# Layer 0: the choice behind GpSimd's norm tile and its last step in two places; the last half's factors on VectorE

## The chip, the cores and the metric

The kernel runs on one core of a Trainium2 chip. A core has five engines that work at the same time: TensorE (PE, with its weight loads as PEld), VectorE (DVE), ScalarE (ACT), GpSimd (POOL) and SyncE (SP), which issues the DMAs here. Each takes its own instructions in order and waits on semaphores for the others. The metric is the time of one execution on the device in microseconds (us), lower is better; shown is the median of several runs.

## The reference

Four pairs of layers work on x of 8 x 512 tokens, 128 wide, all in float32; each adds its result to x, after a norm over the 128 columns. The kernel splits x into 8 batches of 512 tokens. Two of the eight layers are touched.

Layer 0's second half is a mixture of 16 experts with the two best taken, for each token and each of 8 heads (16 columns each):

```python
h = x @ Wm + bm
t = h.reshape(bs * L_ * H, HD)
logits = t @ expert_emb
w = jax.nn.softmax(logits, axis=-1)
topw, topi = jax.lax.top_k(w, K)
hmid = jax.nn.gelu(jnp.einsum('td,edi->tei', t, W1) + b1, approximate=False)
eo = jnp.einsum('tei,eio->teo', hmid, W2) + b2
sel = jnp.take_along_axis(eo, topi[:, :, None], axis=1)
comb = (sel * topw[:, :, None]).sum(axis=1)
return comb.reshape(bs, L_, d) @ Wo + bo
```

Layer 3's second half rounds its inputs to a 4-bit grid in blocks of 16 values, each block with a factor of its own:

```python
scale = jnp.maximum(jnp.max(jnp.abs(xb), axis=-1, keepdims=True) / 6.0, 1e-12)
xn = xb / scale
idx = jnp.searchsorted(_MID, jnp.abs(xn))
q = _GRID[idx] * jnp.sign(xn) * scale
...
gate = fp4_linear(x, w_gate)
y = fp4_linear(x, w_up)
h = jax.nn.silu(gate) * y
return fp4_linear(h, w_down)
```

## The kernel before

The order of the instructions on every engine is the order in which the program writes them (a manual schedule). Layers 0 and 1 run first, then layers 2 and 3 together in one long loop of frames, and the last batch of layer 3 after it, written out by hand in `end()`.

**Layer 0, pass two.** A list of stages, each with a lag, is run for i from -4 to 10, and a stage works on batch i + lag. `turned` (L365-370) turns a normed batch on TensorE and copies it on ScalarE; `scale` (L353-358) norms a batch, three tiles of 128 tokens on ScalarE and the fourth on GpSimd (L358); `stats` gets the norm's factors, with three small operations on GpSimd (L246, L247, L763); `biased` (L361) adds a bias to a whole batch on GpSimd; `spikes` multiplies on GpSimd (L401); `logits` (L445, L446) and `attended` (L274) are VectorE's; `exponentials` is ScalarE's (L449). `keep_clock(n)` (L840) puts n matmuls without a use on TensorE.

**The choice.** `choice(b)` (L451-496) is a generator: it finds the best two of 16 experts for each token and head, with a yield after each step. Most steps are one VectorE instruction on 128 x 512 (L458 to L479); two of them have one on GpSimd behind them (L469, L473). The last steps write the weights: four products, one for each of 128 tokens (L484), in one step; then a transpose on VectorE (L489) and four DMAs to DRAM (`plain`, L492). For batch 0 it is advanced three steps at a time by `chosen(3)` in pass two; `chosen(20)` behind it takes what is left.

**Layer 0, the loop.** 128 units (8 batches x 16 experts) follow. `first_half` makes a hidden activation: matmuls, then two gelus on ScalarE (L594, L595). `second_half`, two units later, multiplies back on TensorE, takes the weights `gs` on VectorE (L607) and adds on GpSimd (L611). `gs` is loaded by SP: a block is four experts, in eight DMAs; `twice` writes the weights of a batch to DRAM twice (`gates`), three units after its choice was stored, and the blocks are read from there; only block 0 of batch 0 comes from `plain` itself, in 16 DMAs. Three buffers hold blocks. The matmuls of `second_half` share one PSUM bank, which L607 frees.

After each `second_half`, `side("V", n)` advances one step of a generator (in units 0 to 5: 4, 2, 1, 2, 1 and 2 steps): the choice of the next batch, if its time has come (from unit 16(b-1)-9 on; batch 1 at once), or else `others()`, which makes layer 1's index tables (`places`) and the norm of layer 1's first batches (`first_norms`). When a generator ends, that takes a slot too. The last step of `first_norms` turns batch 0 on TensorE (L826) and copies it on VectorE (L828); it waits at "P", the slot ahead of the second half, which there is in units 0 to 127 alone. What is left is run behind the loop. Layer 1 begins with the projection of this batch.

**The end.** Batch 7 of layer 3 is done in two halves, A (tokens 0 to 255) and B (256 to 511); L is batch 6, of which the last parts lie among theirs. For each tile of 128 tokens, `gated` multiplies by the gate's and the up weights and takes a tanh on ScalarE (L2158); `gated_v` forms the product on VectorE (L2164), and, with `at_end` and `thirds`, copies the other factor on ScalarE (L2161) and takes the last product on GpSimd (L2166), without `thirds` on VectorE (L2168). `quant_h1` (L1401 to L1406) gets the blocks' factors; `fp4_round` (L1409-1429) rounds: two instructions make a mask (L1418, L1421), one adds it, one subtracts it (L1422, L1423), and GpSimd multiplies by the factors (L1424). `turn_h` turns on TensorE (L2216) and copies on ScalarE (L2219), `down` multiplies back into one PSUM bank, adds to x on VectorE (L2100) and stores by SP (L2239). `bank()` hands out two PSUM banks in turn (tag "one"); `bank("c")` is one of its own, which half A's convolution used before.

Of the kernel before, what the change touches and what calls it, by code (L numbers as in the profile page):

```python
# [17 lines left out]
F32 = mybir.dt.float32  # L18
I32 = mybir.dt.int32
# [145 lines left out]
def body(ctx, tc, dram, spans, x_in, ib, it, ic, ei, out):  # L165
# [23 lines left out]
    def bank(tag="one"):  # L189
        if tag == "one" and "own" in banks:  # L190
            return banks["own"]
        return banks["pool"].tile([P, TB], F32, tag=tag, name="ps1", bufs=banks["tags"][tag])
# [94 lines left out]
    def layer0():  # L287
# [7 lines left out]
        with ExitStack() as st:  # L295
# [64 lines left out]
            def biased(b, bias):  # L360
                nc.gpsimd.tensor_tensor(  # L361
                    x[b], x[b], bc[bias].unsqueeze(1).to_broadcast([P, J, D]), ALU.add
                )
# [87 lines left out]
            def choice(b):  # L451


                d = by_expert(depth, b)
                ex = acc[b].rearrange("p (g e) -> p g e", e=16)
                place, top, sm = small("place"), small("top"), small("sm")
                eq, one, left = big("eq"), big("one"), big("left")
                nc.vector.scalar_tensor_tensor(eq, d, 0.0, rank, ALU.is_equal, ALU.mult)  # L458
                yield "V"
                nc.vector.tensor_reduce(place, eq, AX.X, ALU.max)  # L460
                yield "V"
                nc.vector.tensor_tensor(one, eq, over(place), ALU.is_equal)
                yield "V"
                nc.vector.scalar_tensor_tensor(left, one, -1e30, d, ALU.mult, ALU.add)
                yield "V"
                nc.vector.tensor_reduce(top, left, AX.X, ALU.max)
                yield "V"
                nc.vector.tensor_tensor(eq, left, over(top), ALU.is_equal)
                nc.gpsimd.tensor_tensor(eq, eq, rank, ALU.mult)  # L469
                yield "V"  # L470
                nc.vector.tensor_reduce(sm, ex, AX.X, ALU.add)
                nc.vector.reciprocal(sm, sm)
                nc.gpsimd.tensor_tensor(ex, ex, over(sm), ALU.mult)  # L473
                yield "V"
                nc.vector.tensor_reduce(place, eq, AX.X, ALU.max)
                yield "V"
                nc.vector.tensor_tensor(one, eq, over(place), ALU.is_equal)
                yield "V"
                nc.vector.scalar_tensor_tensor(left, one, -1e30, left, ALU.mult, ALU.add)  # L479
                yield "V"  # L480
                by_e = one.rearrange("p g e -> p (g e)").rearrange("p (j e h) -> p j h e", j=J, h=8)
                for j in range(J):
                    r = slice(8 * j, 8 * (j + 1))
                    nc.vector.scalar_tensor_tensor(  # L484
                        by_e[:, j, :, :], left[:, r, :], -1e29, ex[:, r, :], ALU.is_le, ALU.mult
                    )
                yield "V"
                g = big("turned").rearrange("p g e -> p (g e)")
                nc.vector.transpose(g, one.rearrange("p g e -> p (g e)"))  # L489
                to = plain[b].rearrange("(c r) (j a s) -> a r j c s", c=4, j=J, a=4)  # L490
                for a in range(4):
                    nc.sync.dma_start(  # L492
                        to[a], g[32 * a : 32 * (a + 1), :].rearrange("r (j c s) -> r j c s", j=J, c=4)
                    )
                (written.add if b == 0 else stored.setdefault)(b)
                yield "V"
# [8 lines left out]
            def chosen(n):  # L505
                for _ in range(n):
                    next(first_choice, None)

            with (
                tc.tile_pool(name="a0h", bufs=1) as hp,  # L510
                tc.tile_pool(name="a0", bufs=2) as ap,
                psum({"one": 8}),
                tc.manual_schedule(),
            ):
                hs = [hp.tile([P, NB, TB], F32, tag=f"h{k}", name=f"h{k}") for k in range(3)]
                bst = [hp.tile([P, NB, 6], F32, tag=f"bst{k}", name=f"bst{k}") for k in range(3)]

                def run(stages, iterations):
                    for i in iterations:
                        for f, lag in stages:  # L520
                            if 0 <= i + lag < NB:
                                f(i + lag)

                run(
                    (
                        (scale, 2),
                        (stats, 3),
                        (turned, 1),
                        (project, 0),
                        (lambda b: biased(b, "bp"), -2),  # L530
                    ),
                    range(-3, NB + 2),
                )
                keep_clock(22)
                sc, bi = batch_norm()
                expand()
                run(
                    (
                        (turned, -2),
                        (scale, -1),  # L540
                        (turn_v, 3),
                        (logits, -3),
                        (attended, 0),
                        (stats, 0),
                        (spikes, 4),
                        (gram, 2),
                        (gram_out, 1),
                        (hidden, -2),
                        (exponentials, -3),
                        (lambda b: chosen(3), -4),  # L550
                        (lambda b: biased(b, "bo"), -1),
                        (lambda b: keep_clock(6), -3 - NB // 2),
                    ),
                    range(-4, NB + 3),
                )
                chosen(20)
# [852 lines left out]
    def fp4_round(pool, dst, sc, a, blocks, room=None):  # L1409

        shape = [P, blocks, 16]
        room = room or blocks
        m = pool.tile([P, room, 16], F32, tag=f"fm{room}", name="fm")[:, :blocks, :]
        nc.vector.tensor_scalar(  # L1418
            m.bitcast(I32), a.bitcast(I32), 0x7F800000, None, ALU.bitwise_and
        )  # L1420
        nc.vector.tensor_scalar(m, m, 1.0, 1.5 * 2.0**22, ALU.max, ALU.mult)  # L1421
        nc.vector.tensor_tensor(a, a, m, ALU.add)  # L1422
        nc.vector.tensor_tensor(a, a, m, ALU.subtract)  # L1423
        nc.gpsimd.tensor_tensor(  # L1424
            dst.rearrange("p (n k) -> p n k", k=16),
            a,
            sc.unsqueeze(2).to_broadcast(shape),
            ALU.mult,
        )
# [3 lines left out]
    def late():  # L1433
# [11 lines left out]
        with tc.tile_pool(name="a2", bufs=2) as wp, tc.tile_pool(name="l3", bufs=1) as lp:  # L1445
# [584 lines left out]
            def layer3(b, xp, tile_, part=(0, J), conv_bank="one", h_tag="h"):  # L2030
# [68 lines left out]
                def added(ps):  # L2099
                    nc.vector.tensor_tensor(  # L2100
                        x[b][:, j0:j1, :],
                        x[b][:, j0:j1, :],
                        ps[:, lo:hi].rearrange("p (j d) -> p j d", d=D),
                        ALU.add,
                    )
# [78 lines left out]
                def quant_h2(i):  # L2184
                    fp4_round(lp, pair(i), *t["fh", i], 44)

                def quant_h2_tile(i, j):
                    sc, a = t["fh", i]
                    k = slice(22 * j, 22 * (j + 1))
                    h = tile_("h", h_tile)  # L2190
                    fp4_round(lp, h[:, 2 * i + j, :], sc[:, k], a[:, k, :], 22)

                def blocks_h(i):
                    m = lp.tile([P, 44, 16], F32, tag="fm44", name="hb")
# [26 lines left out]
                        )  # L2221

                def down():
                    ht = tile_("ht", None)
                    po = bank()
                    for j in range(j0, j1):
                        for k, _ in thirds:
                            mm(
                                cols(po, j),
                                ht[:C3, j, k, :],  # L2230
                                wt["down"][:C3, k, :],
                                start=(j == j0 and k == 0),
                                stop=(j == j1 - 1 and k == 2),
                            )
                    added(po)
                    stored()

# [147 lines left out]
            def end():  # L2385
# [48 lines left out]
                B.quant_x1()  # L2434
                A.gated_v(1)
                B.quant_x2()
                L.down()
                keep_clock(6)
                B.turn_x()
                B.gated(2, True)  # L2440
                B.gated(3, True)
                A.quant_h1(0)
                A.quant_h2(0)
                B.gated_v(2)
                B.gated_v(3)
                keep_clock(8)
                B.quant_h1(1)
                A.turn_h(0)
                B.quant_h2_tile(1, 0)
                B.quant_h2_tile(1, 1)  # L2450
                A.down()
                keep_clock(22)
                B.turn_h(1)
                B.down()

# [290 lines left out]
```

## Time and profile before

| | |
|---|---|
| median of 3 runs | 1390.49 us (1388.63 to 1393.59) |
| the profiled execution | 1387.75 us, its span 1385.6 us |
| instructions | 33142 |
| busy: PE, DVE, ACT, POOL | 1323.9, 1024.1, 1011.0, 646.3 us |
| pass two of layer 0 | about 44 to 101 us |
| loop of layer 0 | 101 to 380 us: PE 273.75 and ACT 270.45 busy of 280 |
| the end, from the last frame on | about 1323 to 1385.6 us |

The profile is of one execution. Busy shares are averages over stages with different limits, so each stage is read by itself: the timeline of an engine lists its instructions with start, duration and, in brackets, the time that the engine was idle before and what ended it. A busy PE is not PE at its peak, as its matmuls' ends are modelled.

### The profile page before, as it was taken

The numbers are of one execution on the slowest core, as the hardware profiler recorded it, in microseconds if no ns is written. First come the engines' busy times: TensorE is split into PE (matmuls) and PEld (weight loads), VectorE is DVE, ScalarE is ACT, GpSimd is POOL, SyncE is SP. The second block draws the span as 40 slices with busy tenths as digits, with TensorE's granted clock in tenths as the row PEclk, the third lists the DMA queues.
The fourth block names the chain that finished last, engine by engine and source line by source line (L and its number), as shares of the span: only waits on it lengthen the run. The fifth ranks groups of instructions, "written<-read, shape, count | busy, mean of one in ns | idle before, by whom it ended". The sixth has DMA issues, their size and how long they took to land.

```text
span 1385.6 us, 33142 instructions
## 1 busy us (share of the span) xinstructions
PE 1323.9 (96%) x12910; PEld 704.4 (51%) x12910; DVE 1024.1 (74%) x2173; ACT 1011.0 (73%) x2050; POOL 646.3 (47%) x758
## 2 busy tenths in 40 slices
PE   7889999999989899999999999999999999999997
PEld 3762222222277655547447455555555555555576
DVE  6786666677477778863783689788788897887876
ACT  6859999999977656655684686777767767667632
POOL 6756667765632533230472453453443634424432
PEclk9999999999999999999999999999999999999999
DMA  5015555555280111241201101102011010110000
GB/s 181 1 25 163 170 145 149 150 152 145 62 278 28 28 40 35 65 115 30 73 21 36 45 2 22 31 2 43 11 23 23 9 33 20 23 23 10 2 9 16
DMA packets 125309, 84.47 MB, mean 61 GB/s; under 512 B 61984, under 2 KB 103712, under 8 KB 124769
## 3 DMA queue, kind: packets, MB, share of 16 engines
q1 hardware_dynamic: 123423, 78.43, 20.3%
q0 software_dynamic: 1152, 2.36, 0.6%
q8 instruction: 102, 1.67, 0.5%
q10 hardware_dynamic: 578, 1.57, 0.3%
q14 instruction: 54, 0.44, 0.1%
HBM read 64.29 MB, written 22.23 MB: 62 GB/s over the span
## 4 chain that ended last, share of the span: by engine, by line
PE 37%; DVE 14%; ACT 10%; issue 2%; POOL 1%; DMA 0%; DVEq 0%; ACTq 0%; POOLq 0%
PE ps L250 27%; PE ps L1598 8%; ACT ex L1677 6%; DVE nm L1671 5%; ACT prod L2065 2%; DVE acc L2051 1%; PE ps L2248 1%; DVE fa L1422 1%; DVE fa L1406 1%; ACT q L1559 1%; DVE fsc L1401 1%; ACT xn L1481 1%; DVE fa L1423 1%; DVE fm L1418 1%; DVE k L1560 1%
## 5 line engine op out<-in xcount | busy, mean ns | idle before, releaser
L1677 ACT ACTIVATE ex<-ps,nm 128x512 f32<-128x512 f32 x512 | 345.2, 687 | 172.3 <-DVE nm L1671 172.2
L1671 DVE TENSOR_REDUCE nm<-ps 128x2 f32<-128x1024 f32 x256 | 300.9, 1210 | 39.1 <-PE ps L250 39.0
L250 PE MATMUL ps<-q,k 64*64 64x512 f32 (+1 forms) x2240 | 258.3, 564 | 8.9 <-ACT ex L1677 5.7
L250 PE MATMUL ps<-ex,vs 128*64 128x512 f32 x1024 | 233.8, 598 | 1.1 <-DVE sm L1691 1.1
L1692 POOL TENSOR_TENSOR vs<-v,sm 128x256 f32<-128x256 f32 x128 | 78.6, 614 | 292.9 <-DVE sm L1691 268.6
L1598 PE MATMUL ps<-xt,blob_a 64*64 64x512 f32 x912 | 207.8, 589 | 0.1
L611 POOL TENSOR_TENSOR acc<-acc,pr 128x512 f32<-128x512 f32 x120 | 165.9, 1382 | 87.2 <-DVE pr L607 78.8
L595 ACT ACTIVATE hm<-ps,blob_f 128x1536 f32<-128x1536 f32 x128 | 196.2, 1533 | 0.0
L607 DVE SCALAR_TENSOR_TENSOR pr<-ps,blob_f,gs 128x512 f32<-128x512 f32 x120 | 90.0, 750 | 87.2 <-PE ps L250 76.6
L250 PEld LDWEIGHTS ps<-q,k 64*64 64x64 f32 x2240 | 74.8, 132 | 152.0 <-ACT ex L1677 78.2
L250 PE MATMUL ps<-h,w 32*128 32x512 f32 x1024 | 148.3, 643 | 1.1 <-ACT hm L594 0.6
L250 PEld LDWEIGHTS ps<-ex,vs 128*64 128x64 f32 x1024 | 68.0, 136 | 152.9 <-issue 128.1
L250 PE MATMUL ps<-hm,w 128*32 128x512 f32 x1024 | 136.8, 606 | 5.1 <-DVE pr L607 2.7
L2066 POOL TENSOR_TENSOR acs<-acs,prod 128x512 f32<-128x512 f32 x96 | 124.0, 1292 | 23.9 <-ACT prod L2065 19.4
L1598 PE MATMUL ps<-blob_a,ct 64*64 64x128 f32 x1824 | 118.6, 269 | 0.0
L1598 PE MATMUL ps<-blob_a,xt 64*64 64x128 f32 x1824 | 118.5, 269 | 0.0
L1598 PEld LDWEIGHTS ps<-blob_a,ct 64*64 64x64 f32 x1824 | 106.2, 133 | 0.0
L1677 ACT ACTIVATION_READ_ACCUMULATOR ex<-ps,nm 128x1 f32 x512 | 105.0, 205 | 0.0
L1598 PEld LDWEIGHTS ps<-blob_a,xt 64*64 64x64 f32 x1824 | 103.0, 133 | 0.0
L250 PEld LDWEIGHTS ps<-h,w 32*128 32x128 f32 x1024 | 41.1, 183 | 108.7 <-ACT hm L594 103.4
L594 ACT ACTIVATE hm<-ps,blob_f 128x512 f32<-128x512 f32 x128 | 88.0, 687 | 8.5 <-PE ps L250 8.3
L1598 PEld LDWEIGHTS ps<-xt,blob_a 64*64 64x64 f32 x912 | 61.7, 133 | 31.9 <-issue 28.4
(366 smaller groups left out, 2212.3 us busy)
## 6 DMA issues: line engine op xcount, KB each, us to landing
gs<-gates SPq DMA_DIRECT2D x248, 128.0 KB, 3.0
gates<-plain SPq DMA_DIRECT2D x16, 256.0 KB, 3.2
ht<-turned_h SPq DMA_DIRECT2D x20, 180.0 KB, 2.8
turned_h<-hb SPq DMA_DIRECT2D x40, 88.0 KB, 2.3
blob_f<-in_f SPq DMA_DIRECT2D x1, 2560.0 KB, 9.2
blob_a<-in_a SPq DMA_DIRECT2D x1, 2056.0 KB
x<-in_x SPq DMA_DIRECT2D x8, 256.0 KB, 5.7
plain<-turned SPq DMA_DIRECT2D x32, 64.0 KB, 2.2
```

The lines of the kernel that those rows point to most:

```text
L250: nc.tensor.matmul(out_, lhs, rhs, start=start, stop=stop)
L594: nc.scalar.activation(hm[:, 0, :], p1, AF.Gelu, bias=bias)
L595: nc.scalar.activation(hm[:, 1:, :], p3, AF.Gelu, bias=bias)
L607: nc.vector.scalar_tensor_tensor(pr, po, f0["b2"][:, e : e + 1], gs, ALU.add, ALU.mult)
L611: nc.gpsimd.tensor_tensor(acc[b], acc[b], pr, ALU.add)
L1401: nc.vector.tensor_reduce(sc, s3, AX.X, ALU.max, apply_absolute_value=True)
L1598: ins = nc.tensor.matmul(*args, **kw).ins
L1671: nc.vector.tensor_reduce(nm, ps, AX.X, ALU.max, negate=True)
L1677: nc.scalar.activation(ex[kt][:, i, :], ps[:, i, :], AF.Exp, bias=nm[:, i : i + 1], accum_out=sm[:, kt, i : i + 1],)
L1692: nc.gpsimd.tensor_tensor(vs[:, tiles, :, :], vs_[n][:, tiles, :].rearrange("p j (i n) -> p j i n", i=2), sm[:, tiles, :].unsqueeze(3).to_ ...
L2065: nc.scalar.activation(p, src, AF.Copy, scale=w)
L2066: nc.gpsimd.tensor_tensor(t["acs"], t["acs"], p, ALU.add)
```

## The change

In pass two, batch 0's choice and the second bias move from the end of an iteration to the place behind `scale` in the next one (their lags are one lower, so that each works on the same batch as before). The choice's step of four products becomes two steps of two products, so that a choice has 13 steps and no longer 12; this holds for all eight batches.

In `end()`, batch 6's `down` is split: `down_products` (its matmuls, into bank "c") and `down_out` (the addition to x and the store). The matmuls move behind half B's products, where `keep_clock(8)` was, the addition and the store behind half A's `down`. `keep_clock(6)` becomes 17 and the last one 13 instead of 22. Half B's `gated` takes both products on VectorE. Its last rounding goes from two calls for a tile each (masks on 22 blocks) to `quant_h2_pair`: the masks on all 44 blocks at once, then for each tile add, subtract and multiply, the multiply of the first tile on GpSimd and of the second on VectorE.

```diff
@@ -484,7 +484,8 @@
                     nc.vector.scalar_tensor_tensor(
                         by_e[:, j, :, :], left[:, r, :], -1e29, ex[:, r, :], ALU.is_le, ALU.mult
                     )
-                yield "V"
+                    if j % 2:
+                        yield "V"
                 g = big("turned").rearrange("p g e -> p (g e)")
                 nc.vector.transpose(g, one.rearrange("p g e -> p (g e)"))
                 to = plain[b].rearrange("(c r) (j a s) -> a r j c s", c=4, j=J, a=4)
@@ -538,6 +539,8 @@
                     (
                         (turned, -2),
                         (scale, -1),
+                        (lambda b: chosen(3), -5),
+                        (lambda b: biased(b, "bo"), -2),
                         (turn_v, 3),
                         (logits, -3),
                         (attended, 0),
@@ -547,8 +550,6 @@
                         (gram_out, 1),
                         (hidden, -2),
                         (exponentials, -3),
-                        (lambda b: chosen(3), -4),
-                        (lambda b: biased(b, "bo"), -1),
                         (lambda b: keep_clock(6), -3 - NB // 2),
                     ),
                     range(-4, NB + 3),
@@ -2184,11 +2185,23 @@
                 def quant_h2(i):
                     fp4_round(lp, pair(i), *t["fh", i], 44)
 
-                def quant_h2_tile(i, j):
+                def quant_h2_pair(i):
                     sc, a = t["fh", i]
-                    k = slice(22 * j, 22 * (j + 1))
-                    h = tile_("h", h_tile)
-                    fp4_round(lp, h[:, 2 * i + j, :], sc[:, k], a[:, k, :], 22)
+                    m = lp.tile([P, 44, 16], F32, tag="fm44", name="fm")
+                    nc.vector.tensor_scalar(
+                        m.bitcast(I32), a.bitcast(I32), 0x7F800000, None, ALU.bitwise_and
+                    )
+                    nc.vector.tensor_scalar(m, m, 1.0, 1.5 * 2.0**22, ALU.max, ALU.mult)
+                    for j, engine in enumerate((nc.gpsimd, nc.vector)):
+                        k = slice(22 * j, 22 * (j + 1))
+                        nc.vector.tensor_tensor(a[:, k, :], a[:, k, :], m[:, k, :], ALU.add)
+                        nc.vector.tensor_tensor(a[:, k, :], a[:, k, :], m[:, k, :], ALU.subtract)
+                        engine.tensor_tensor(
+                            tile_("h", h_tile)[:, 2 * i + j, :].rearrange("p (n k) -> p n k", k=16),
+                            a[:, k, :],
+                            sc[:, k].unsqueeze(2).to_broadcast([P, 22, 16]),
+                            ALU.mult,
+                        )
 
                 def blocks_h(i):
                     m = lp.tile([P, 44, 16], F32, tag="fm44", name="hb")
@@ -2221,8 +2234,10 @@
                         )
 
                 def down():
+                    down_out(down_products(bank()))
+
+                def down_products(po):
                     ht = tile_("ht", None)
-                    po = bank()
                     for j in range(j0, j1):
                         for k, _ in thirds:
                             mm(
@@ -2232,6 +2247,9 @@
                                 start=(j == j0 and k == 0),
                                 stop=(j == j1 - 1 and k == 2),
                             )
+                    return po
+
+                def down_out(po):
                     added(po)
                     stored()
 
@@ -2434,22 +2452,21 @@
                 B.quant_x1()
                 A.gated_v(1)
                 B.quant_x2()
-                L.down()
-                keep_clock(6)
+                keep_clock(17)
                 B.turn_x()
-                B.gated(2, True)
-                B.gated(3, True)
+                B.gated(2, True, False)
+                B.gated(3, True, False)
                 A.quant_h1(0)
                 A.quant_h2(0)
                 B.gated_v(2)
                 B.gated_v(3)
-                keep_clock(8)
+                po = L.down_products(bank("c"))
                 B.quant_h1(1)
                 A.turn_h(0)
-                B.quant_h2_tile(1, 0)
-                B.quant_h2_tile(1, 1)
+                B.quant_h2_pair(1)
                 A.down()
-                keep_clock(22)
+                L.down_out(po)
+                keep_clock(13)
                 B.turn_h(1)
                 B.down()
```

## The prediction

> **What bounds the kernel now.** I read the page's table of slices first, then the timeline engine by engine at the places that the change touches: pass two (68 to 101 us), layer 0's loop (101 to 377), the handoff to layer 1 (377 to 395) and the end (1355 to the last write). In the table ScalarE and TensorE both stand at 9 through the loop, so there whatever stops ScalarE is time. These are rows of ScalarE's timeline in the loop (start, duration, operation; in brackets the idle time before it and who ended it):
>
> ```profile
> 122.29 0.69 ACT L594 ACTIVATE hm<-ps,blob_f 128x512 f32<-128x512 f32 x1 [1.23 <-PE ps L250]
> ...
> 147.83 0.69 ACT L594 ACTIVATE hm<-ps,blob_f 128x512 f32<-128x512 f32 x1 [0.41 <-PE ps L250]
> 150.99 0.69 ACT L594 ACTIVATE hm<-ps,blob_f 128x512 f32<-128x512 f32 x1 [1.04 <-PE ps L250]
> 182.45 0.69 ACT L594 ACTIVATE hm<-ps,blob_f 128x512 f32<-128x512 f32 x1 [0.41 <-PE ps L250]
> ```
>
> A unit takes 2.07 us and ScalarE rests only here and there. VectorE's rows before 147.83 show why:
>
> ```profile
> 142.21 0.75 DVE L607 SCALAR_TENSOR_TENSOR pr<-ps,blob_f,gs 128x512 f32<-128x512 f32 x1 [0.72 <-PE ps L250]
> 142.88 2.10 DVE L484 SCALAR_TENSOR_TENSOR one<-left,acc 128x128 f32<-128x128 f32 x4
> 144.82 0.72 DVE L607 SCALAR_TENSOR_TENSOR acc<-ps,blob_f,gs 128x512 f32<-128x512 f32 x1
> ```
>
> The four products of a choice's last step fill VectorE's whole gap, the next L607 comes at 144.82 instead of 144.28 (142.21 plus 2.07), TensorE waits for its bank, ScalarE for TensorE.
>
> Pass two is VectorE's: from 68.8 to 94.9 it has no idle time. Two of its steps are stretched by GpSimd:
>
> ```profile
> 73.63 1.27 POOL L361 TENSOR_TENSOR x<-x,blob_bc 128x512 f32<-128x512 f32 x1
> 74.01 1.43 DVE L462 TENSOR_TENSOR one<-eq,place 128x512 f32<-128x512 f32 x1
> 74.89 0.88 POOL L358 TENSOR_SCALAR xn<-x,rs,nb 128x128 f32<-128x128 f32 x1
> ...
> 86.06 1.06 POOL L473 TENSOR_TENSOR acc<-acc,sm 128x512 f32<-128x512 f32 x1
> 86.45 1.21 DVE L477 TENSOR_TENSOR one<-eq,place 128x512 f32<-128x512 f32 x1
> 87.08 1.71 POOL L361 TENSOR_TENSOR x<-x,blob_bc 128x512 f32<-128x512 f32 x1
> ```
>
> L462 takes 0.69 alone (102.25); here it ends 0.54 after GpSimd's 74.90. So a VectorE step with two inputs in SBUF waits for the GpSimd instruction under way, and, as L361's 1.71 shows, the one that waits goes before GpSimd's next.
>
> The end is one chain, mostly VectorE and GpSimd:
>
> ```profile
> 1362.72 0.69 DVE L2100 TENSOR_TENSOR x<-x,ps 128x512 f32<-128x512 f32 x1
> ...
> 1370.28 1.81 POOL L2166 TENSOR_TENSOR h<-s,prod 128x352 f32<-128x352 f32 x2
> 1372.12 0.89 DVE L1401 TENSOR_REDUCE fsc<-h 128x44 f32<-128x704 f32 x1 [2.47 <-POOL h L2166]
> ...
> 1379.31 0.98 PE L2216 MATMUL ps<-blob_c,h 128*120 128x128 f32 x6 [1.25 <-DVE x L2100]
> ```
>
> The last transposes wait for VectorE's L2100, which frees their PSUM bank.
>
> **Pass two: -1.55 us.** VectorE's order stays, since turned and scale put nothing on it; only GpSimd's changes: L358 now comes ahead of the choice's L469 and L473 and of L361. L462, ready at 74.01, meets L358 (0.45 from 73.67) instead of L361, waits 0.1 and then goes before L361: 0.65 saved. L477 likewise meets L358 rather than L473: 0.5 saved. TensorE's wait of 2.41 us for L358 at 84.36 goes too, worth nothing by itself, as VectorE is behind. So stats of batch 7 are 1.15 earlier. Behind them xt of batch 7 stands on ScalarE behind exponentials of batch 5, which waited for L446 until 94.90. The transpose (0.71 at 92.88) now lies after L446, so another 0.4 goes, and hidden of batch 7 (96.09) and all to the loop's first matmul come 1.55 earlier. Bounds: if VectorE gains nothing, 0.33 (the transpose alone); at most 1.9. The transpose's four DMAs then go out at 93.8 (before, 93.62), as VectorE's gain nearly pays for the step it slips. Each thing behind them on SP follows: sixteen of gs, two of gates, eight of gs for block 1 (0.593 each from 110.38, 3.0 to land, so there at 117.5). L607 of unit 4 came at 119.30, behind four products and the transpose; now the transpose is after it, it could go at 117.1 and waits for gs until 117.65: 1.65 earlier. The loop is **-1.65** ahead from here. If VectorE gained nothing, the store would be 1.31 late, gs there at 118.85, and this term -0.4.
>
> **The split in the loop: -2.49 us.** Of the four products, the first two ended by 143.48; the third began at 143.34, met L611 on GpSimd (143.11 to 144.50) and took 1.42. Two a unit take about 0.65 and end before that. ScalarE's rests of 0.41 to 0.42 before 147.83, 182.45, 217.07, 250.60, 284.14 and 317.80 go: 3 x 0.41 + 3 x 0.42. If both halves met L611, they would end 1.65 after the product, with about 0.2 left at each of two units, so the term would be nothing. Each choice now holds 13 slots. Its stores move one unit (two for batch 2); gates of a batch are written three units on, and the block that reads them is issued at 16(b-1)+9 against 16(b-1)+6 or 7, so no SP queue decides there.
>
> **The turn of batch 0: -0.80, then +0.96.** With 13 slots, and one more for the end of each choice, the side generator of layer 1 loses seven. I counted the yields: before, its transposes come at n=121 (361.65, and ScalarE rests 0.80 at 364.46); now it stands at "P" when the loop ends, and the transposes run after the last unit.
>
> ```profile
> 378.73 1.06 PE L250 MATMUL ps<-hm,w 128*32 128x512 f32 x8
> 379.72 1.13 PE L250 MATMUL ps<-xt,blob_l 128*128 128x512 f32 x2
> ...
> 382.13 0.60 ACT L880 ACTIVATE ex<-ps 128x512 f32<-128x512 f32 x1 [2.16 <-POOL acc L611]
> 383.29 0.58 ACT L880 ACTIVATE ex<-ps 128x512 f32<-128x512 f32 x1
> ```
>
> In the loop's old times: transposes at 379.72 (0.66), VectorE's copy (0.69) behind its L607, to 381.29; the projection of q at 381.35 instead of 379.72, of k at 382.3 to 384.2, and the exponential of k, at 383.29 before, at 384.25: +0.96. From there k, gather and the next projection follow one another each iteration, so it stays. Bounds: 0.42 (the first exponential, which waited for L611 anyway) and 1.63 (TensorE's whole delay).
>
> **The end: -1.35 us.** The write of batch 6 leaves the chain: quant_h1(0) starts at 1362.72 instead of 1363.41, and its 5.39 end at 1368.11. The halves' L2166 on GpSimd (up to 1372.10) become four VectorE products of 0.53, to 1370.23. quant_h1(1) takes 2.53 (1372.12 to 1374.65), to 1372.76; the two masks on 44 blocks 1.12 (1365.85 to 1366.97), to 1373.88; add and subtract 0.56 each, to 1375.0. Now GpSimd's multiply (0.79) and VectorE's next three meet as in pass two: add to 1375.55, GpSimd to 1376.4, subtract to 1376.95, multiply (half of 0.9 and the fixed part, 0.54) to 1377.5. The release by A's L2100 comes at 1377.85, the transposes at 1378.0 instead of 1379.31. keep_clock(17) ends at 1363.57 (34 matmuls of 0.1125 from 1359.74), when xq is there; L.down's 24 matmuls fill the place of keep_clock(8), and its L2100 (0.69) and 256 KB write lie after the release, beside ScalarE and TensorE. Bounds: -2.1 if GpSimd and VectorE don't meet; +0.8 if the clock falls (rival two).
>
> **Sum:** -1.65 - 2.49 - 0.80 + 0.96 - 1.35 = -5.33 us. The profiled execution took 1387.75 (span 1385.60, 2.15 around it), below the lowest of the three runs (1388.63) and 2.74 below their median; the difference goes onto the median: 1390.49 - 5.33 = **1385.2 us**.
>
> **Rivals.** *One, GpSimd and VectorE meet again in pass two in other places* (slower). L358 and L361 now lie right beside the choice's steps, of which five have two SBUF inputs; were each held by one L361 (1.27), 6.35 come instead of the 1.26 held now, and the 1.65 is lost: 1385.2 + 1.65 + 5.09 = **1391.9**. It decides once L361 starts before VectorE's step in four of the five; against it, a waiting VectorE went first at 74.90 and 87.12. 7%.
>
> *Two, the clock at the end.* TensorE now rests from 1375.3 to 1378.0. Granted clock in stretches of pass two:
>
> ```profile
> 82.00:84.00 2.00, 0.00 (x0) 0.00 (x0) 1.97 (x6) 0.90 (x2) 2.00 (x3) 1.00 0.00 0
> ...
> 85.00:86.00 1.00, 1.00 (x6) 1.00 (x6) 0.97 (x3) 0.36 (x1) 0.92 (x2) 0.50 0.00 0
> ```
>
> After a rest of 2.41 us the clock (third number from the right) was 0.50, and eight matmuls took 1.75 instead of 1.16. The last transposes (0.53) and twelve matmuls (1.62) would double: +2.15, so **1387.4**. The Trainium skill ("TensorE: Matmul & The Clock Gate", Part 1: The HAM clock gate) has the clock fall after an idle window of about 3.4 us; by that the rest of 2.7 is harmless and the sum stays 1385.2. This trace shows a fall after less, in a window that 2.41 filled only partly, so it hangs on how the window lies. 20%.
>
> *Three, pass two gives only the transpose's place*, -0.4 for -1.65: **1386.4**. For it: GpSimd still has all its work in the same stretch. 18%.
>
> *Four, the split does nothing* (both halves meet L611): **1387.7**. Against it, the rows of the first two products. 8%.
>
> **How the numbers follow.** My forecast has 47%, with 1383 to 1387.5 as its own range. For all cases the low end is the best bounds (-1.9, -2.49, -0.80, +0.42, -2.1: 1383.6) less 2 for the spread of three runs; the high end takes in rivals two to four with the same spread: 1381.6 to 1390. About 0.3% (4.2 us, so 1386.3) is what can be told from no change: 0.8 of the forecast, a little under half of two and three and little of four lie below it: faster 0.58, same 0.35, slower 0.07 (rival one and what I haven't seen).
>
> **What would show it.** L462 and L477 at 0.7 to 0.8, first gelu near 101.3; no 0.4 rests of ScalarE at the batches; L826 after the last L607 and q's projection 1.6 behind it; L2216 of the last half about 5 us earlier, clock 1.00. I am wrong if steps of the choice stay above 1 us, if 0.50 stands near the end, or if layer 1 loses more than 1.6 us.

## The result and the profile after

The changed kernel took 1385.84 us (median of 8 runs, 1385.05 to 1387.24) against 1390.55 of the kernel before in the same set (8 runs, 1388.63 to 1394.82): ratio 0.9963, 95% interval 0.9949 to 0.9978, 4.71 us less. The forecast was 5.33 less. In a second set of runs it was 1383.97 (12 runs) against 1388.18 (35 runs), ratio 0.9976 (0.9967 to 0.9984). The profiled execution took 1385.33 us, its span 1383.6; what lies just ahead of pass two came 1.04 us earlier in it than in the profile of before (no part of the change is there), so differences of place below are taken after 1.04 is set aside, and "in before's times" means with 1.04 added. From layer 0 on, the changed kernel's lines count one higher than before's (L607 is L608, L594 is L595), in `end()` 13 higher.

**Pass two**, timelines of GpSimd and VectorE (start, duration, operation; idle time before it and who ended it):

```profile
72.79 0.45 POOL L358 TENSOR_SCALAR xn<-x,rs,nb 128x128 f32<-128x128 f32 x1
72.98 0.80 DVE L462 TENSOR_TENSOR one<-eq,place 128x512 f32<-128x512 f32 x1
73.20 1.70 POOL L361 TENSOR_TENSOR x<-x,blob_bc 128x512 f32<-128x512 f32 x1
...
84.88 0.79 DVE L477 TENSOR_TENSOR one<-eq,place 128x512 f32<-128x512 f32 x1
85.10 1.49 POOL L473 TENSOR_TENSOR acc<-acc,sm 128x512 f32<-128x512 f32 x1
```

VectorE's two steps fell from 1.43 and 1.21 to 0.80 and 0.79; now GpSimd's instruction is the one that is held (1.70 for 1.27, 1.49 for 1.06). The loop's first matmul came at 98.71 instead of 101.05: 1.30 of it is the change's.

**Unit 4 of the loop**, VectorE before and after (the products of units 3 and 4 before; of units 1, 3 and 4, with the choice's step between, after):

```profile
115.85 0.75 DVE L607 SCALAR_TENSOR_TENSOR pr<-ps,blob_f,gs 128x512 f32<-128x512 f32 x1 [0.66 <-PE ps L250]
...
119.30 0.71 DVE L607 SCALAR_TENSOR_TENSOR pr<-ps,blob_f,gs 128x512 f32<-128x512 f32 x1
```

```profile
110.48 0.75 DVE L608 SCALAR_TENSOR_TENSOR pr<-ps,blob_f,gs 128x512 f32<-128x512 f32 x1 [1.46 <-PE ps L250]
...
115.06 0.75 DVE L608 SCALAR_TENSOR_TENSOR pr<-ps,blob_f,gs 128x512 f32<-128x512 f32 x1 [0.66 <-PE ps L250]
115.72 2.11 DVE L484 SCALAR_TENSOR_TENSOR one<-left,acc 128x128 f32<-128x128 f32 x4
117.67 0.72 DVE L608 SCALAR_TENSOR_TENSOR pr<-ps,blob_f,gs 128x512 f32<-128x512 f32 x1
```

The lead of 1.30 doesn't last. Unit 1's product waits 1.46 for TensorE, and unit 3's comes 0.25 later than before (116.10 for 115.85, in before's times). Unit 4's product comes 0.59 earlier (118.71 for 119.30), since it now stands ahead of the batch's transpose. It waits for nothing: the last of the block's eight loads had landed at 116.55.

**The loop**, ScalarE and VectorE:

```profile
146.06 1.53 ACT L596 ACTIVATE hm<-ps,blob_f 128x1536 f32<-128x1536 f32 x1
148.97 0.69 ACT L595 ACTIVATE hm<-ps,blob_f 128x512 f32<-128x512 f32 x1 [1.37 <-PE ps L250]
...
183.45 0.69 ACT L595 ACTIVATE hm<-ps,blob_f 128x512 f32<-128x512 f32 x1 [1.37 <-PE ps L250]
262.30 0.69 ACT L595 ACTIVATE hm<-ps,blob_f 128x512 f32<-128x512 f32 x1 [0.26 <-PE ps L250]
362.26 0.69 ACT L595 ACTIVATE hm<-ps,blob_f 128x512 f32<-128x512 f32 x1 [0.24 <-PE ps L250]
```

```profile
142.98 0.62 DVE L484 SCALAR_TENSOR_TENSOR one<-left,acc 128x128 f32<-128x128 f32 x2
144.46 0.75 DVE L608 SCALAR_TENSOR_TENSOR pr<-ps,blob_f,gs 128x512 f32<-128x512 f32 x1 [0.86 <-PE ps L250]
145.13 1.68 DVE L484 SCALAR_TENSOR_TENSOR one<-left,acc 128x128 f32<-128x128 f32 x2
146.91 0.69 DVE L274 TENSOR_TENSOR x<-x,ps 128x512 f32<-128x512 f32 x1
```

The six rests of 0.41 and 0.42 are gone. But the two at the `finish` of a batch were 1.04 and are 1.37, and there are two new ones, of 0.26 and 0.24. Batch 2's second pair of products met GpSimd's addition after all (1.68 for 0.62); the other five choices' pairs took 0.62 or 0.63.

**The handoff**, TensorE and ScalarE: the turn of batch 0 (L827) runs behind the last second half, and q's projection waits for VectorE's copy of it.

```profile
374.45 1.06 PE L250 MATMUL ps<-hm,w 128*32 128x512 f32 x8
375.45 0.66 PE L827 MATMUL ps<-blob_c,xn 128*128 128x128 f32 x4
377.06 1.13 PE L250 MATMUL ps<-xt,blob_l 128*128 128x512 f32 x2 [0.95 <-DVE xt L829]
```

**The end**, VectorE and TensorE:

```profile
1375.34 0.52 DVE L2197 TENSOR_TENSOR fa<-fa,fm 128x352 f32<-128x352 f32 x1
1375.89 0.99 DVE L2198 TENSOR_TENSOR fa<-fa,fm 128x352 f32<-128x352 f32 x1
1376.98 0.53 DVE L2199 TENSOR_TENSOR h<-fa,fsc 128x352 f32<-128x352 f32 x1
1377.42 1.01 DVE L2101 TENSOR_TENSOR x<-x,ps 128x256 f32<-128x256 f32 x2
1379.98 0.42 DVE L2101 TENSOR_TENSOR x<-x,ps 128x256 f32<-128x256 f32 x1 [1.54 <-PE ps L250]
```

```profile
1376.55 0.54 PE L2229 MATMUL ps<-blob_c,h 128*120 128x128 f32 x3 [0.68 <-POOL h L2199]
1377.89 0.54 PE L2229 MATMUL ps<-blob_c,h 128*120 128x128 f32 x3 [0.80 <-DVE x L2101]
```

Two rows of before beside them:

```profile
1376.90 0.81 DVE L1421 TENSOR_SCALAR fm<-fm 128x352 f32<-128x352 f32 x1
1382.03 0.42 DVE L2100 TENSOR_TENSOR x<-x,ps 128x256 f32<-128x256 f32 x1 [2.87 <-PE ps L250]
```

One VectorE instruction is held beside GpSimd's multiply (0.99 for 0.53), as one was before (0.81 for 0.34). The transposes, which all six waited for the bank before, go in two threes: the first tile's wait for its data alone. The whole run stood 0.54 late ahead of the end, against the profile of before, and the last addition comes at 1379.98 instead of 1382.03: -2.59.

**The clock** in stretches of the loop's start and of the end (bounds; sum of the windows; busy time of PE, PEld, DVE, ACT, POOL; granted TensorE clock, DMA share, GB/s):

```profile
99.40:102.80 3.40, 2.51 (x18) 0.65 (x10) 3.24 (x5) 3.39 (x4) 0.00 (x0) 0.99 0.39 107
102.80:106.20 3.40, 3.40 (x16) 1.11 (x16) 0.00 (x0) 2.67 (x4) 1.27 (x1) 0.50 0.50 148
106.20:109.60 3.40, 3.40 (x20) 0.72 (x16) 1.69 (x3) 1.58 (x2) 0.50 (x1) 0.51 0.50 156
...
1375.00:1378.40 3.40, 1.93 (x16) 1.50 (x16) 3.26 (x6) 0.48 (x1) 0.93 (x1) 1.00 0.00 0
```

At the end it holds at 1.00. At the loop's start it is at half for two windows.

### The profile page after: what moved, and what is told of

It reads as the page before. It is cut to its first block, busy times and chain, and to the rows that moved or that the text cites. A ratio compares the mean times of both kernels' runs of the same rounds, so it can differ in the third digit from the quotient of the medians.

```text
span 1383.6 us, 33116 instructions
## 1 busy us (share of the span) xinstructions
PE 1322.8 (96%) x12898; PEld 702.4 (51%) x12898; DVE 1020.8 (74%) x2174; ACT 1010.7 (73%) x2048; POOL 644.6 (47%) x755
## 4 chain that ended last, share of the span: by engine, by line
PE 37%; DVE 15%; ACT 10%; issue 2%; POOL 0%; DMA 0%; DVEq 0%; ACTq 0%; POOLq 0%
PE ps L250 27%; PE ps L1599 8%; ACT ex L1678 6%; DVE nm L1672 5%; ACT prod L2066 2%; DVE acc L2052 1%; PE ps L2266 1%; DVE fa L1423 1%; DVE fa L1407 1%; DVE fsc L1402 1%; ACT q L1560 1%; ACT xn L1482 1%; DVE k L1561 1%; DVE fa L1424 1%; DVE fm L1419 1%
## 5 line engine op out<-in xcount | busy, mean ns | idle before, releaser
L608 DVE SCALAR_TENSOR_TENSOR pr<-ps,blob_f,gs 128x512 f32<-128x512 f32 x120 | 90.0, 750 | 87.8 <-PE ps L250 71.8
L595 ACT ACTIVATE hm<-ps,blob_f 128x512 f32<-128x512 f32 x128 | 88.1, 688 | 6.7 <-PE ps L250 6.5
```

Source lines behind the costliest of these rows:

```text
L595: nc.scalar.activation(hm[:, 0, :], p1, AF.Gelu, bias=bias)
L608: nc.vector.scalar_tensor_tensor(pr, po, f0["b2"][:, e : e + 1], gs, ALU.add, ALU.mult)
```

## What one execution's time is made of

The runs of one kernel differ by more than the change is worth. Each comes with its mean granted clock, and the 82 runs of the kernel before in the experiments' three sets lie on a line by it:

| mean clock | runs | median us |
|---|---|---|
| 1.000 | 21 | 1386.31 |
| 0.999 | 11 | 1386.81 |
| 0.998 | 11 | 1387.62 |
| 0.997 | 16 | 1388.58 |
| 0.996 | 12 | 1390.18 |
| 0.995 | 10 | 1392.06 |
| 0.993 | 1 | 1395.46 |

A straight line through all 209 runs of all kernels (one constant for each kernel and set, one slope) gives 1.04 us for each 0.001 of missing clock. In the profiles the clock falls to 0.50 in whole windows of 3.41 us, which lie on another phase in each execution; before's profile has them at 84.69 and 105.17, the changed kernel's at 102.73 (two in a row) and 464.55. So below a kernel is given with its median and, from this fit, its distance to before at equal clock. The second is an estimate, and too good for a kernel whose windows at half clock lie where TensorE is not the bound. Fitted to each kernel by itself, the slope lies between 0.3 and 1.4, so a difference of 0.002 in clock leaves about 1 us open. And where an edit itself brings the windows, their time is part of what it costs.

## The experiments

Each set is measured beside the kernel before, each on a chip of its own: 1387.66 (32 runs) for the first four, 1388.18 (35) for the next four, 1388.47 (15) for the last four.

| kernel | median us | ratio to before, 95% | at equal clock |
|---|---|---|---|
| layer 0 alone | 1387.28 | 0.9988 (0.9976 to 1.0000) | -3.1 |
| end alone | 1383.62 | 0.9970 (0.9955 to 0.9986) | -3.0 |
| split alone | 1389.45 | 1.0013 (1.0003 to 1.0023) | -1.0 |
| lags alone | 1388.97 | 1.0004 (0.9991 to 1.0017) | -0.8 |
| changed, again | 1383.97 | 0.9976 (0.9967 to 0.9984) | -6.2 |
| gates early | 1384.68 | 0.9973 (0.9962 to 0.9984) | -6.3 |
| turn in the tail | 1382.49 | 0.9965 (0.9953 to 0.9976) | -7.6 |
| bank o | 1384.19 | 0.9969 (0.9957 to 0.9981) | -6.4 |
| clock fill | 1382.08 | 0.9963 (0.9948 to 0.9977) | -6.5 |
| fill and gates | 1377.93 | 0.9930 (0.9915 to 0.9944) | -8.8 |
| all together | 1381.37 | 0.9955 (0.9940 to 0.9969) | -8.7 |
| factors on GpSimd | 1384.51 | 0.9970 (0.9955 to 0.9985) | -5.3 |

**Layer 0 alone, end alone.** The diff's hunks of layer 0, or those of `end()`, each on the kernel before.

> Both edits of layer 0, the end as it was before. Theory, from the trace of the changed kernel: pass two -1.4, the split -1.3, the turn of batch 0 -0.8 in the loop and +1.0 behind it, so 2.5 us less than before; ScalarE's rests before the gelu are 1.37 twice and none of 0.41; the last half's first transposes still wait for VectorE's addition. Rival: what layer 0 gains is lost again at the row gathers of layers 2 and 3 (VectorE's waits near 668 and 786 us were 2.7 longer), so the time is within 0.7 us of before's.

> The edits of the end, layer 0 as it was before. Theory: the end gives -2.7 us, as the two traces show when they are laid on each other behind 1357 us, of which -1.35 is VectorE's and GpSimd's chain and the rest the first tile's transposes, which no longer wait for the bank; the first three transposes start with the GpSimd product, the last three with VectorE's addition of half A. Rival: only the chain (-1.35) and the rest belongs to chance in one execution: then -1.4, with all six transposes behind the addition.

The end alone gives most: 4.0 between the medians, and -2.57 at the end when its trace is laid on before's. Its three lines there are those of the changed kernel:

```profile
1379.13 0.55 PE L2228 MATMUL ps<-blob_c,h 128*120 128x128 f32 x3 [0.68 <-POOL h L2198]
1380.47 0.54 PE L2228 MATMUL ps<-blob_c,h 128*120 128x128 f32 x3 [0.80 <-DVE x L2100]
```

The bank's part isn't chance, then, and the rival of -1.4 falls. Layer 0 alone is 0.4 below before, and neither the theory's 2.5 nor the rival's mechanism: VectorE's waits near 667 and 782 us are 1.58 in its profile, as before. By its trace the edits are worth -2.3 up to layer 1, and a window at half clock at 467.5 takes 2.0 of it. The mean clock is 0.9961 over its 12 runs, against 0.9979 for before in this set.

**Split alone, lags alone.**

> The choice's last step in two places, the lags and the end as before. Theory: the rests of 0.41 go, but the two at the finish of a batch grow from 1.04 to 1.37, since the matmuls of the finish then wait for ScalarE's gelu to free their bank: -1.8 in the loop less up to 0.5 for late weights, -0.8 and +1.0 for the turn of batch 0, and -0.3 in pass two for the transpose behind the logits: -1.5 to -2 in all. Rival (as predicted): the split gives 2.5 with rests of 1.04 left as they were. Second rival: both halves meet GpSimd's addition and the rests of 0.4 stay.

> The lags alone, the choice in 12 steps, the end as before. Theory: VectorE's two held steps of pass two (1.43 and 1.21) fall to about 0.8, so the loop's first matmul comes 1.0 us earlier; the transpose of batch 0 stays ahead of the logits, so the 0.4 of its place isn't gained; the loop is as before, with six rests of 0.41 and two of 1.04, and the turn of batch 0 inside it: -1.0 in all. Rival: GpSimd's multiplies and additions meet other VectorE steps and the loop starts less than 0.4 earlier.

```diff
-                yield "V"
+                    if j % 2:
+                        yield "V"
```

```diff
+                        (lambda b: chosen(3), -5),
+                        (lambda b: biased(b, "bo"), -2),
...
-                        (lambda b: chosen(3), -4),
-                        (lambda b: biased(b, "bo"), -1),
```

Neither is faster than before. Laid on before up to layer 1, the traces give -1.4 for the lags and -0.4 for the split. The split's has a window at half clock at 119.65 that takes 1.65 (units 4 to 6 take 5.73, and 4.08 in layer 0 alone); without it the split would give -2.1. The mean clocks are 0.9957 with the split and 0.9965 with the lags. In the traces both do what was expected in the loop: with the split, rests of 1.37 twice and 0.26, 0.24 at the same places as in the changed kernel (so the latter two are fixed, not chance; the first stands at an expert 7, not at a new block of weights, so "late weights" was wrong, and what holds VectorE there is open); without it, six of 0.41 to 0.43, two of 1.03 and 1.04, and 0.80 for the turn. The lags bring the loop's first step 1.0 forward, the split alone 0.3 (99.53 against 101.05, with all ahead 1.18 earlier). But what the loop does with an early start is seen at its unit 4, where VectorE waits for the next block of weights:

```profile
114.28 2.11 DVE L484 SCALAR_TENSOR_TENSOR one<-left,acc 128x128 f32<-128x128 f32 x4
116.42 0.71 DVE L489 STREAM_TRANSPOSE turned<-one 128x512 f32<-128x512 f32 x1
118.06 0.75 DVE L607 SCALAR_TENSOR_TENSOR pr<-ps,blob_f,gs 128x512 f32<-128x512 f32 x1 [0.93 <-DMA gs<-gates]
```

(This is the end alone, layer 0 as before.) From batch 0's transpose to this product of unit 4 it is 26.42 us before, 26.02 with the end alone, 24.80 with the split, 25.89 with the lags, 25.53 with both, 25.66 in the changed kernel. In the end alone, the split, the lags and both edits the product starts 0.28 behind the landing of the block's last load: there a chain of DMAs binds, which begins with the transpose, whatever the loop's first matmul does. Before and in the changed kernel that load had landed 1.49 and 1.12 ahead of the product, which follows VectorE's own work at once. Laid on before, unit 4 comes 0.73 earlier with both edits (119.03 against 119.30, all ahead 0.46 later).

**The changed kernel again.**

> The changed kernel once more, with a second profile. Theory: the time of one execution is the kernel's own plus about 1.1 us for each 0.001 of granted clock missing, so at equal clock it is 4 us below before; VectorE's waits near 668 and 786 us (3.94 and 2.56 in the first profile) belong to that execution and are 1.58 here, as in before. Rival: they belong to the change and are there again.

VectorE's waits are 1.58 and 1.58, as before: the first profile's 3.94 and 2.56 were of that execution (2.7 us), and perhaps of its set, whose constant at equal clock is 2.3 higher.

**Gates early.** The weights of batch 0 are written twice between the halves of block 0's loads.

> The changed kernel with the two DMAs that write batch 0's weights twice put between the two halves of the sixteen loads of block 0. Theory: the loop's unit 4 is bound by the chain of weight DMAs that begins with batch 0's transpose (24.8 to 26.4 us from there to unit 4's product in six executions, however early the loop's first matmul is), so the second block lands 2.5 us sooner, unit 4's product no longer waits for it and comes 22.5 to 24 us behind the transpose: -2 us. Rival: VectorE's choice of batch 1 and TensorE set unit 4 by themselves: then less than 0.5.

```diff
                             nc.sync.dma_start(
                                 gs[16 * hd : 16 * (hd + 1), e : e + 2, :],
...
-                    twice(0)
+                        if e == 0:
+                            twice(0)
```

The second block's loads go out at 107.33 instead of 109.07, yet unit 4's product comes at 118.03, no sooner, and it waits for no DMA: TensorE is at half clock for two windows from 103.24 on, as in the changed kernel. The theory of one bound falls; there are two.

**Turn in the tail, bank o.**

> The changed kernel with the turn of batch 0 put behind the first half of the last unit, into a bank of its own, where TensorE has no more first halves to do. Theory: the handoff's +1.0 goes and the loop's 0.8 doesn't come back: -1.0, q's projection again right behind the last second half. Rival: layer 1's first exponential is held by the last addition on GpSimd and by the finish anyway: -0.4 or less.

> The changed kernel with the last half's second tile turned into bank 'o', which nothing uses any more, where it had the bank that VectorE's addition of half A frees. Theory: its three transposes start with VectorE's product of that tile (ready 0.4 before they start now): -0.3 us at the end. Rival: they wait for ScalarE's copy or the weights' load: 0.

```diff
+                        else:
+                            banks["own"] = threes[0][:, 1, :]
+                            side("P", n)
+                            banks.pop("own")
```

```diff
-                        pt = bank()
+                        pt = bank(own) if own and j % 2 else bank()
...
-                B.turn_h(1)
+                B.turn_h(1, "o")
```

```profile
373.03 0.66 PE L831 MATMUL ps<-blob_c,xn 128*128 128x128 f32 x4
374.04 1.07 PE L250 MATMUL ps<-hm,w 128*32 128x512 f32 x8 [0.35 <-DVE pr L608]
...
377.12 1.13 PE L250 MATMUL ps<-xt,blob_l 128*128 128x512 f32 x2
```

The turn lies between second halves, q's projection comes at once behind the last, and the trace gains 1.02 between 374 and 387 us. With bank o the last three transposes wait for their own data (1376.52, "0.47 <-DVE h L2199"), and the last addition comes 0.33 earlier against the rest of the trace; 0.3 can't be seen in a median here.

**Clock fill, fill and gates.** Unused matmuls behind the first halves of units 0 and 1.

> The changed kernel with eight and six unused matmuls behind the first halves of the loop's first two units. Theory: all five profiles of the changed kernel's pass two have TensorE at 0.50 for two windows from 102.8 to 104.8 us on, since in the window before it has only matmuls of 32 rows; with full matmuls among them the clock stays at 1.00 there; unit 4 is then bound by the chain of weight DMAs instead, which ends as late, so the time falls by less than 0.5 us. Rival: the clock falls all the same.

> The same fill, and batch 0's weights written twice between the two halves of block 0's loads. Theory: two bounds end at the same time at unit 4, the chain of DMAs and TensorE at half clock; either alone gave nothing, both together give -2 us: unit 4's product comes 23 us behind batch 0's transpose instead of 25.7. Rival: a third bound (VectorE with batch 1's choice) lies as near: less than 0.7.

```diff
                     first(n)
+                    if n < 2:
+                        keep_clock(4 - n)
```

The fill alone, VectorE:

```profile
113.41 2.10 DVE L484 SCALAR_TENSOR_TENSOR one<-left,acc 128x128 f32<-128x128 f32 x4
117.58 0.75 DVE L608 SCALAR_TENSOR_TENSOR pr<-ps,blob_f,gs 128x512 f32<-128x512 f32 x1 [2.07 <-DMA gs<-gates]
```

Fill and early gates, VectorE, and the clock in stretches:

```profile
113.02 2.10 DVE L484 SCALAR_TENSOR_TENSOR one<-left,acc 128x128 f32<-128x128 f32 x4
114.96 0.72 DVE L609 SCALAR_TENSOR_TENSOR pr<-ps,blob_f,gs 128x512 f32<-128x512 f32 x1
```

```profile
99.40:102.80 3.40, 3.40 (x26) 1.80 (x19) 3.23 (x5) 3.37 (x5) 0.00 (x0) 1.00 0.38 106
102.80:106.20 3.40, 3.40 (x30) 1.36 (x29) 0.70 (x2) 3.40 (x5) 1.27 (x1) 1.00 0.80 227
```

This settles the loop's start (the changed kernel has no runs in this third set; its figures are those of the second). With the fill alone the clock stays at 1.00 and VectorE waits 2.07 for the weights instead (the median is 1.9 lower than the changed kernel's, more than expected, but at equal clock only 0.3: its mean clock is 0.9978; its trace has 0.7 at unit 4, -1.31 for -0.59); with the early gates alone the clock stands in the way; with both, unit 4's product comes 22.7 behind the transpose and nothing waits ahead of it but VectorE's own products. It is the best of all kernels run: 0.9930 (0.9915 to 0.9944) of before, 6 us below the changed kernel's median; 2.6 of them are there at equal clock, the rest is clock that isn't missing (0.9994, five runs).

**All together.** The two, the turn, bank o, and `keep_clock(4)` and `keep_clock(2)` about the row gather's transposes in layer 1.

> All that helped or should help, together: the fill, the early weights, the turn in the tail (-1.0), bank 'o' (-0.3), and eight and four unused matmuls at the row gather near 463 us, where five of six profiles with the split have a window at 0.50 that costs 1 to 2 us. Theory: -4.5 us against the changed kernel, 1379.5 or less. Rival: the parts don't add, as the clock falls somewhere else: 1381 to 1382.5.

Each part shows in its trace (-3.2 to unit 4, -1.0 at the handoff, no half clock at 461 to 467), but windows at half clock stand at 495.12 and 792.08, and the mean clock is 0.9962 against 0.9994 for fill and gates. The rival holds. At equal clock the two are the same; that the turn's 1.0 doesn't show there is open.

**Factors on GpSimd.**

> The changed kernel with the second tile's last multiply on GpSimd too. Theory: the last transposes wait for their bank, which half A's addition on VectorE frees; with the multiply off VectorE that addition comes 0.45 earlier, GpSimd's multiply takes 0.8 to 0.9 in place of 0.53 on VectorE and ends as late as the addition, so the end moves by less than 0.2 us. Rival: the factor on VectorE is what shortens the end: +0.4.

```diff
-                    for j, engine in enumerate((nc.gpsimd, nc.vector)):
+                    for j, engine in enumerate((nc.gpsimd, nc.gpsimd)):
```

```profile
1378.42 0.79 POOL L2199 TENSOR_TENSOR h<-fa,fsc 128x352 f32<-128x352 f32 x1 [0.46 <-DVE fa L2198]
```

It ends at 1379.21, and the last transposes start at 1379.26; laid on the changed kernel's second trace that is 0.1 sooner. The theory holds by the trace (the medians, 0.5 apart, don't tell): the factor on VectorE is worth nothing as long as the bank is the gate, which frees as late as GpSimd's product ends.

## Why the prediction came out

Its sum was -5.33; by the traces the same parts make -0.59 - 1.84 - 0.80 + 1.01 - 2.59 = -4.81, and the medians differ by 4.71. Two terms were too large, by 1.1 and 0.65, and one too small by 1.2, so the total is better than its parts. That it also meets the medians is partly luck: the edits of layer 0 come with more windows at half clock (mean clock 0.9962 over the changed kernel's 20 runs, 0.9977 over before's 82), at some 1.6 us by the fit, and the first set's gathers cost up to 2.7 more.

- **Pass two, forecast -1.65 at unit 4: -0.59.** The held steps were right (0.63 and 0.42 saved, 0.65 and 0.5 forecast), and 1.30 of 1.55 reached the loop's first matmul. The step that failed lies behind it: the lead was to run on to unit 4, whose product could go at 117.1 and would wait for block 1 until 117.65. Block 1 landed as forecast (117.59 in before's times), but TensorE was at half clock for two windows from 102.73 on, where before's profile has one (105.17), and the lead was gone by unit 3's product. The working put the clock at the loop's start at nothing; its rival looked at the end alone. What is left at unit 4 is the product's place ahead of the transpose: 2.61 behind unit 3's, where it was 3.45. The second profile has the same (-0.31, with the load 1.37 ahead of the product). That it is the clock, the fill shows: with 1.00 there unit 4's product comes 1.31 before the old one (117.58, with all ahead 0.41 earlier), and now the chain of DMAs binds. Putting the DMAs right alone gives nothing at this place, keeping the clock alone 0.7, both 3.0.
- **Split, forecast -2.49: -1.84.** All six rests went, 0.46 to 0.48 each by the places of ScalarE's rows. The term left out what the rests had paid: with TensorE 0.41 late, the matmuls of `finish`, which go to the bank that ScalarE's gelu reads, found it free. Without the rest they wait for the gelu:

```profile
180.16 1.13 PE L250 MATMUL ps<-blob_f,acc 128*128 128x128 f32 x8 [0.29 <-ACT hm L596]
```

  That takes back 0.33 at each of two batches; the two new rests take 0.3 each, and a rest of 0.23 at 130.84 went too. With the turn's -0.80 the loop gains 2.65 from unit 4 on, and 2.66 and 2.67 in layer 0 alone and the second profile. Meeting L611 once, as rival four has it, cost nothing visible: batch 3's `finish` rests 1.37 without it.
- **Turn of batch 0, forecast -0.80 and +0.96: -0.80 and +1.01.** Mechanism and size right, and both shown: the turn in the tail takes the 1.02 back.
- **End, forecast -1.35: -2.59.** Mis-sized twice. GpSimd's multiply was to come behind VectorE's add of the second tile; it started beside it (1375.57, the add runs from 1375.34 to 1375.86), so all behind it, to half A's addition that frees the bank, comes 0.5 to 0.65 earlier than worked out. And the first tile's transposes got another bank than the one that waits for that addition, which the working didn't look at: half of the transposes, copies and matmuls are done ahead, 0.6 more. The end alone repeats it (-2.57).
- **Rivals.** One (GpSimd meets VectorE elsewhere) did not come: no step of the choice above 0.80 in pass two. Two: the clock is 1.00 to the last transpose in all profiles with the changed end. Three is nearest to what pass two gave, by another cause. Four fell. The clock was the right thing to fear, but at the loop's start.

The Trainium skill ("TensorE: Matmul & The Clock Gate", Part 1: The HAM clock gate) has a free-running window of 3413 ns and a clock that halves after an idle one. The first agrees (windows of 3.413 us, on another phase in each execution). The second doesn't: the fall at 102.73 follows a window in which TensorE was busy for 2.52 of 3.41 us, all of it in matmuls of 32 rows, and no rest was longer than 0.6; with fourteen unused full matmuls there the clock stayed. Here the measurement decides.

## What to carry to other kernels

When a wait is to go, look for who else lived on the delay: a rest can have paid for the next wait, and an earlier start can run into a chain of DMAs that starts elsewhere. If a mended bound gives nothing, mend it together with the one that stands beside it before you drop it: here, at unit 4, one alone gave nothing, the other 0.7, and both 3.0. With several windows at half clock in a run, compare kernels at equal granted clock and read a small edit's worth at its place in the trace, since the medians can say the opposite (the split alone measures slower, with its mean clock 0.002 below before's).

## What was not expected of the hardware

- Each 0.001 of granted clock missing is 1.04 us here, and explains before's spread from 1385.45 to 1395.46 nearly whole (what is left is 0.8 us, one standard deviation).
- Busy time doesn't tell whether the clock holds. At the loop's start it fell after windows with TensorE busy for 2.52 us (the changed kernel, and before), and stayed after 2.57, 2.57 and 2.75 of the same kind of matmuls (end, split and lags alone). What the falls go with is how much of the array is used. Count a matmul as its rows x columns x length, with 128 x 128 on 512 columns as 1, in windows of 3.413 us on each execution's own phase. From 30 us on, the fourteen traces have 5497 such windows at full clock; each of the 27 ahead of a fall holds 3.08 or less, each of the others 2.99 or more. At the loop's start it is 3.00 in the changed kernel, 2.78 before, 3.49 to 3.76 in the three that stayed, and 5.55 and 5.49 with the unused matmuls.
- The window at half clock near 465 us stands in seven of the eight profiles with the split and without a fill, and in none of the three without the split. It falls where TensorE rests for the row gather's DMA (0.61 in the changed kernel). Before's trace has that rest too (1.02), and a window that began within some 2.3 us there would hold less than 3.05, so the phase alone may have spared it; whether layer 0's order, 90 us earlier, has a part stays open.
